# TensorE's 128-column work gathered into every second stage of a convolution-and-involution kernel

## The chip, the cores and the metric

The kernel runs on one core of one Trainium2 chip. The metric is device microseconds (us) of one execution, the median of several runs. Profiles are one execution each, by the hardware profiler. The engines are called PE (TensorE, the matrix engine; PEld is its weight load), DVE (VectorE), ACT (ScalarE), POOL (GpSimd) and SP (which here only issues DMAs).

## The reference

The input x is 32 images of 256 channels by 32x32 pixels, in float32. Two layers, each with a residual, where gn is a group norm with 32 groups of 8 channels:

```python
# layer 0: 3x3 convolution, 256 -> 256 channels, operands clipped to float16's range
x = x + conv3x3(quantize(gn(x)), quantize(weight)) + bias
# layer 1: involution; every pixel makes its own 7x7 kernel for each of 16 groups of 16 channels
z = gn(x)
y = relu(batchnorm(w1 @ z))               # 256 -> 64 channels, per pixel
w = w2 @ y + b2                           # 64 -> 16 groups * 49 taps, per pixel
x = x + sum over 49 taps of w[group, tap, pixel] * z[channel, pixel shifted by tap]
```

## The kernel before

The images go through a pipeline that is written out by hand: one Python loop (line 513) emits instructions for all engines, and each engine executes its own in the order in which they were emitted. The loop runs over **stages** n. An image has 16 of them: four blocks k of 8 image rows, times two sets v of columns of the 7x7 window (v=0: four columns, 128 partitions; v=1: three columns, 96 partitions), times two halves d of its rows (d=0: four, d=1: three). I number them 0 to 15 by n mod 16; k=0 is stages 0 to 3. In the iteration for stage n are emitted, in this order:

1. the *products* of stage n (`products`, L408): weights times shifted pixels, on DVE into tiles `pa` and `pb` and on POOL into `pg`. `pa` and `pb` have two buffers each, `pg` four;
2. the *sums* of stage n-1 (`sums`, L462): PE matmuls with a 32-column 0/1 matrix `shift`, four side by side in the array, that add the products up into `acc`. A stage with d=0 takes 32 of them in the trace, one with d=1 24, and the corner stages of k=0 fewer;
3. one step of `finish`, which closes a block of rows: ACT copies acc (`ob`, L473), PE transposes it with four 128-column matmuls (L479, in stages 1, 5, 9, 13), DVE adds it to x (L488, L491);
4. in even stages the *weights* for stages n+2 and n+3 (`weights`, L371): small 32-column matmuls into `pw` (64 in the trace for v=0, 48 for v=1), half of which ACT then copies to `ws` (L380) for POOL;
5. one step of every `front` that is running. A front is a generator, one for an image, started 38 stages before the image's stage 0; each `yield` ends a step, and each iteration runs one step of each live front, the oldest first.

A front's steps are these. The first group norm: sums (ACT, L195), means (PE `pg` matmul with `avg`, L203, and ACT, L210), squares (L195), variances (`pg` again, then `s` and `ve` on ACT, L220 and L222), scales (a reciprocal `r` on DVE, L226), and apply, a run of ten small and large ACT instructions (L231 to L243) that writes `xq`. Then the convolution in four units of 18 matmuls (L287, 128x128 weights, 512 columns moving, float16), each spread over four steps by `CONV = (0, 6, 4, 8)`; after a unit come the clip `q` on DVE (L301), `qb` on ACT (L303), the residual `x` on POOL (L305) and ACT's sums of it. Then the second group norm, whose apply writes `xn`; four steps with four transposes each (`pt`, L324), a copy by ACT (`xt4`, L328) and four DMAs (L330) that store the normalized image by pixels in DRAM; `load_pixels` (L359), which loads it to `xpix`; and `py` (L337, 64 columns) with ACT's relu into `y_pad` (L345). The tile `m` in PSUM, which pg, pt and py share, has one buffer.

In the steady state three fronts are live: that of image b+1 is in its second group norm and transposes while b+2 is convolved and b+3 begins. The second norm's variances are emitted in stage 4, its scales and apply in stage 5, the transposes in stages 6, 7, 8 and 9, load_pixels and py in stage 10. The first norm's apply is emitted in stage 0 and the convolution in stages 1 to 15.

Of the kernel before, what the change touches and what calls it, by code (L numbers as in the profile page):

```python
# [57 lines left out]
def tile_quant_conv_then_involution(  # L58
# [28 lines left out]
    def load_x(b):  # L87
        xt = xpool.tile([P, CH, N], F32, tag="x", name=f"x_{b}")
        for h in range(CH):
            nc.sync.dma_start(xt[:, h], x[b, h * P : (h + 1) * P])  # L90
        return xt
# [93 lines left out]
    class GroupNorm:  # L185
# [42 lines left out]
        def apply(self, dst, src):  # L228
# [10 lines left out]
            for h in range(CH):  # L239
# [8 lines left out]
                    scale=rstd[:, one],  # L248
                )


    CONV = (0, 6, 4, 8)

    def front(b):


        xt = x_tiles[b]
        gn = GroupNorm()
        gn.begin(1)
        for h in range(CH):  # L260
            gn.add_up(xt, 0, h, 0, N, AF.Identity)
        yield
        gn.means()
        gn.squares(xt)
        yield
        gn.variances()
        yield
        gn.scales()
        yield
        yield  # L270
        yield

        gn.apply(lambda h: xq[:, h, PAD0 : PAD0 + H, PAD0 : PAD0 + W], xt)
        yield
        gn = GroupNorm()
        gn.begin(N // NT)
        units = [(nt, mh) for nt in range(N // NT) for mh in range(CH)]
        for s in range(1, 4 * len(units) + 3):
            u, i = divmod(s, 4)
            if u < len(units):  # L280
                nt, mh = units[u]
                if i == 1:
                    pc = ps_c.tile([P, NT], F32, tag="pc", name="pc")
                for n in range(sum(CONV[:i]), sum(CONV[: i + 1])):
                    kh, k = divmod(n, K0 * K0)
                    i0, j0 = divmod(k, K0)
                    nc.tensor.matmul(  # L287
                        pc,
                        wq[:, kh, k, mh * P : (mh + 1) * P],
                        xq[:, kh, nt * RT + i0 : nt * RT + i0 + RT, j0 : j0 + W],  # L290
                        start=n == 0,
                        stop=n == CH * K0 * K0 - 1,
                    )

            u, i = divmod(s - 4, 4)
            if 0 <= u < len(units) and i < 3:
                nt, mh = units[u]
                cols = slice(nt * NT, (nt + 1) * NT)
                if i == 0:
                    q = work.tile([P, NT], F16, tag="q", name="q", bufs=1)  # L300
                    nc.vector.tensor_scalar(q, pc, F16_MAX, -F16_MAX, ALU.min, ALU.max)  # L301
                    qb = work.tile([P, NT], F32, tag="qb", name="qb", bufs=1)
                    nc.scalar.activation(qb, q, AF.Identity, bias=bias_sb[:, mh : mh + 1])  # L303
                elif i == 1:
                    nc.gpsimd.tensor_tensor(xt[:, mh, cols], qb, xt[:, mh, cols], ALU.add)  # L305
                else:
                    gn.add_up(xt, nt, mh, nt * NT, (nt + 1) * NT, AF.Identity)
            yield
        gn.means()
        gn.squares(xt)  # L310
        yield
        gn.variances()
        yield
        gn.scales()
        xn = work.tile([P, CH, N], F32, tag="xn", name=f"xn_{b}", bufs=1)
        gn.apply(lambda h: xn[:, h].rearrange("p (r c) -> p r c", c=W), xt)
        yield

        xd = pixels[b] = dram.tile([W, H, C], F32, tag="xd", name=f"xd_{b}")
        for r in range(0, H // 4, 2):  # L320
            pt = ps_m.tile([P, 2, C], F32, tag="m", name="pt")
            for s in range(2):
                for h in range(CH):
                    nc.tensor.transpose(  # L324
                        pt[:, s, h * P : (h + 1) * P], xn[:, h, (r + s) * P : (r + s + 1) * P], ident
                    )
            xt4 = work.tile([P, 2, C], F32, tag="xt4", name="xt4")
            nc.scalar.copy(xt4, pt)  # L328
            for i in range(4):
                nc.sync.dma_start(xd[:, 4 * r + i : 4 * r + i + 5 : 4, :], xt4[i * W : (i + 1) * W])  # L330
            yield
        load_pixels(b, 0)

        py = ps_m.tile([P, NT], F32, tag="m", name="py")
        for kh in range(CH):
            for nt in range(N // NT):
                nc.tensor.matmul(  # L337
                    py[nt * CR : (nt + 1) * CR],
                    w1_sb[:, kh, :],
                    xn[:, kh, nt * NT : (nt + 1) * NT],  # L340
                    start=kh == 0,
                    stop=kh == CH - 1,
                )
        for nt in range(N // NT):
            nc.scalar.activation(  # L345
                y_pad[b % 2][:CR, nt * RT : (nt + 1) * RT, PAD1 : PAD1 + W],
                py[nt * CR : (nt + 1) * CR].rearrange("p (r c) -> p r c", c=W),
                AF.Relu,
                bias=bn_shift,
                scale=bn_scale,  # L350
            )
        yield

    def load_pixels(b, i):

        for r0, r1 in (((0, 7), (15, 22), (7, 15)), ((0, 14), (14, 22)))[i]:
            src = HELD[i][r0]
            for q in range(Q):
                nc.sync.dma_start(  # L359
                    xpix[i][q * W : (q + 1) * W, r0:r1], pixels[b][:, src : src + r1 - r0, :]  # L360
                )
# [92 lines left out]
    def sums(acc, v, d, moves):  # L454
        p = W * len(COLS[v])
        most = max(len(m) for m in moves)
        for i in range(most):
            for t in range(T):
                if i < len(moves[t]):
                    moving, of = moves[t][i]  # L460
                    cols = slice(0, NT) if of == 2 else slice(of * C, (of + 1) * C)
                    nc.tensor.matmul(  # L462
                        acc[t * W : (t + 1) * W, cols],
                        shift[v][:p],
                        moving,
                        start=(v, d, i) == (0, 0, 0),
                        stop=(v, d, i) == (len(COLS) - 1, len(DI) - 1, len(moves[t]) - 1),
                    )
# [39 lines left out]
    with tc.manual_schedule():  # L508
        fronts, done = {}, {}
        ending = iter(())  # L510
        acc = last = None
        pws = {}
        for n in range(FRONT, len(stages) + 3):
            if 0 <= n < len(stages):
                b, k, v, d = stages[n]
                now = stages[n], products(b, k, v, d, *pws[n // 2])
            else:
                now = None
            if last is not None:
                (b, k, v, d), prods = last  # L520
                if (v, d) == (0, 0):
                    acc = ps_acc.tile([P, NT], F32, tag="acc", name="acc")
                sums(acc, v, d, prods)
            next(ending, None)
            if last is not None and (v, d) == (len(COLS) - 1, len(DI) - 1):
                ending = finish(b, k, acc)
                next(ending)
            last = now
            b, at = divmod(n, per)
            if at == 0 and 0 <= b < B:  # L530
                load_pixels(b, 1)
            if 0 <= n + 2 < len(stages) and n % 2 == 0:
                pws.pop(n // 2 - 1, None)
                pws[n // 2 + 1] = weights(*stages[n + 2][:3])
            b, at = divmod(n - LOAD, per)
            if at == 0 and 0 < b < B:
                x_tiles[b] = load_x(b)
            b, at = divmod(n - FRONT, per)
            if at == 0 and 0 <= b < B:
                fronts[b] = front(b)  # L540
                done[b] = 0
            for b in list(fronts):
                due = n - FRONT - b * per + 1
                if b == 1:

                    due = min(due, max(0, 2 * (due - HOLD)))
                while b in fronts and done[b] < due:
                    if next(fronts[b], fronts) is fronts:
                        fronts.pop(b)
                    done[b] += 1  # L550


# [34 lines left out]
```

## Time and profile before

| | us |
|---|---|
| median of 3 runs | 2783.15 (2783.02 to 2784.85) |
| the profiled execution | 2785.05 |
| its span, first to last instruction | 2783.3 |
| PE, POOL, DVE, ACT busy | 2721.5, 2576.7, 2478.3, 1048.0 |
| from one image's py to the next one's, image after image | 84.25 |

The granted PE clock is 0.991 over the span. "Busy" of PE is the union of its matmuls, whose ends are modelled and overlap, so starts are a better guide: the text that follows goes by the starts of matmuls in the timeline. A merged row of the timeline gives the start of the first instruction, the time from there to the end of the last one, the instruction and how many.

### The profile page before, as it was taken

To read this page: it belongs to the slowest core of one execution; us is meant where nothing else is said; L and a number is where in the kernel's file an instruction comes from. 1 tells how busy PE (TensorE), PEld (TensorE's weight loads), DVE (VectorE), ACT (ScalarE), POOL (GpSimd) and SP (SyncE) were. 2 spreads that over 40 slices of the span, in tenths; PEclk is the share of its full clock that TensorE was granted. 3 is DMA by queue.
4 is the path that set the end of the run, shared out by engine and by line. 5 is a ranking of instruction groups with operands and counts; after the bars stand their busy time and mean duration, and the time that the engine had idled before them with its cause. 6 is when DMAs were issued, how large, how long until landed. Compare 5 with 4: busy or idle time off the path is not lost.

```text
span 2783.3 us, 73320 instructions
## 1 busy us (share of the span) xinstructions
PE 2721.5 (98%) x32320; PEld 1222.7 (44%) x32320; DVE 2478.3 (89%) x1451; ACT 1048.0 (38%) x2179; POOL 2576.7 (93%) x857
## 2 busy tenths in 40 slices
PE   5999999999999999999999999999999999999998
PEld 2444444444444444444444444444444444444443
DVE  1799999999999999999999999999999999999898
ACT  5443344343343433343433343433433433434210
POOL 2799999999999999999999999999999999999997
PEclk8999999999999999999999999999999999999999
DMA  2555434355344454343454343454343453443440
GB/s 94 116 121 128 99 89 116 96 121 122 96 100 104 107 122 113 94 111 91 116 126 109 89 118 87 121 128 98 90 115 96 122 121 96 102 102 93 107 115 16
DMA packets 99853, 292.60 MB, mean 105 GB/s; under 512 B 21389, under 2 KB 62349, under 8 KB 86990
## 3 DMA queue, kind: packets, MB, share of 16 engines
q1 hardware_dynamic: 99534, 287.93, 42.5%
q8 instruction: 252, 4.13, 0.7%
q14 instruction: 67, 0.55, 0.1%
HBM read 220.73 MB, written 67.11 MB: 103 GB/s over the span
## 4 chain that ended last, share of the span: by engine, by line
PE 90%; ACT 4%; issue 2%; POOL 2%; DMA 1%; DVE 1%; POOLq 0%; SPq 0%; ACTq 0%; DVEq 0%
PE acc L462 50%; PE pc L287 18%; PE pw L371 13%; PE pt L324 2%; PE py L337 2%; PE acc L479 2%; POOL pg L408 2%; PE pg L203 1%; ACT xq L243 1%; ACT qb L303 1%; ACT w L234 1%; DMA xpix<-xd 0%; DVE pa L408 0%; ACT u L236 0%; ACT off L242 0%
## 5 line engine op out<-in xcount | busy, mean ns | idle before, releaser
L408 POOL TENSOR_TENSOR pg<-ws,xpix 96x2048 f32<-96x2048 f32 (+2 forms) x704 | 2407.0, 3451 | 23.5 <-PE acc L462 17.6
L408 DVE TENSOR_TENSOR pa<-pw,xpix 128x4096 f32<-128x4096 f32 (+7 forms) x832 | 2006.2, 2446 | 223.1 <-ACT junk L195 86.9
L462 PE MATMUL acc<-pa,shift 128*32 128x512 f32 (+3 forms) x7680 | 1566.2, 570 | 6.9 <-DVE pa L408 6.8
L462 PE MATMUL acc<-pg,shift 128*32 128x512 f32 (+1 forms) x5248 | 1481.5, 599 | 6.3 <-POOL pg L408 6.3
L462 PEld LDWEIGHTS acc<-pa,shift 128*32 128x32 f32 (+1 forms) x7680 | 379.2, 110 | 807.4 <-issue 764.6
L287 PE MATMUL pc<-xq,wq 128*128 128x512 f16 x2304 | 576.8, 387 | 18.7 <-ACT xq L243 15.5
L462 PE MATMUL acc<-pb,shift 128*32 128x512 f32 (+1 forms) x1152 | 531.1, 597 | 0.8 <-DVE pb L408 0.8
L371 PEld LDWEIGHTS pw<-w_sb,y 65*32 65x32 f32 x14336 | 415.0, 110 | 140.6 <-issue 134.4
L371 PE MATMUL pw<-w_sb,y 65*32 65x112 f32 x14336 | 442.7, 260 | 0.0
L380 ACT COPY ws<-pw 128x448 f32<-128x448 f32 (+1 forms) x256 | 135.9, 531 | 724.7 <-PE pw L371 715.3
L462 PEld LDWEIGHTS acc<-pg,shift 128*32 128x32 f32 (+1 forms) x5248 | 354.9, 110 | 65.2 <-issue 51.2
L287 PEld LDWEIGHTS <-wq 128*128 128x128 f16 x2304 | 213.5, 99 | 311.1 <-issue 119.9
L408 DVE TENSOR_TENSOR pb<-pw,xpix 128x1536 f32<-128x1536 f32 x192 | 335.0, 1745 | 0.0
L305 POOL TENSOR_TENSOR x<-qb,x 128x512 f32<-128x512 f32 x128 | 164.4, 1285 | 169.7 <-ACT qb L303 154.4
L473 ACT COPY ob<-acc 128x512 f32<-128x512 f32 x128 | 75.1, 587 | 515.9 <-PE acc L462 514.5
L328 ACT COPY xt<-pt 128x512 f32<-128x512 f32 x128 | 75.0, 586 | 227.0 <-PE pt L324 125.8
L195 ACT ACTIVATE junk<-x 128x512 f16<-128x512 f32 (+1 forms) x192 | 147.9, 770 | 10.7 <-POOL x L305 6.2
L195 ACT ACTIVATE junk<-x,mean 128x1024 f16<-128x1024 f32 x128 | 147.2, 1150 | 4.1
L462 PEld LDWEIGHTS acc<-pb,shift 128*32 128x32 f32 (+1 forms) x1152 | 111.2, 109 | 8.5 <-issue 4.3
L301 DVE TENSOR_SCALAR q<-pc 128x512 f16<-128x512 f32 x128 | 87.0, 680 | 31.3 <-PE pc L287 31.3
L479 PEld LDWEIGHTS acc<-ident,ob 128*128 128x128 f32 x512 | 53.6, 140 | 108.1 <-issue 82.2
L303 ACT ACTIVATE qb<-q,bias_sb 128x512 f32<-128x512 f16 x128 | 92.5, 722 | 11.8 <-DVE q L301 11.8
(51 smaller groups left out, 975.1 us busy)
## 6 DMA issues: line engine op xcount, KB each, us to landing
xpix<-xd SPq DMA_DIRECT2D x256, 256.0 KB, 10.0
xpix<-xd SPq DMA_DIRECT2D x256, 224.0 KB, 5.1
xpix<-xd SPq DMA_DIRECT2D x128, 448.0 KB, 6.6
x<-in_x SPq DMA_DIRECT2D x64, 512.0 KB, 3.6
xd<-xt SPq DMA_DIRECT2D x512, 64.0 KB, 1.7
out<-x SPq DMA_DIRECT2D x32, 640.0 KB, 3.1
out<-x SPq DMA_DIRECT2D x32, 384.0 KB, 2.5
wf<-in_w SPq DMA_DIRECT2D x2, 1152.0 KB, 8.7
```

The costliest lines, as they stand in the source:

```text
L195: nc.scalar.activation(junk[:, n0:n1], src[:, h, n0:n1], func, bias=bias, accum_out=self.sums[:, part, h : h + 1])
L287: nc.tensor.matmul(pc, wq[:, kh, k, mh * P : (mh + 1) * P], xq[:, kh, nt * RT + i0 : nt * RT + i0 + RT, j0 : j0 + W], start=n == 0, stop=n ...
L301: nc.vector.tensor_scalar(q, pc, F16_MAX, -F16_MAX, ALU.min, ALU.max)
L303: nc.scalar.activation(qb, q, AF.Identity, bias=bias_sb[:, mh : mh + 1])
L305: nc.gpsimd.tensor_tensor(xt[:, mh, cols], qb, xt[:, mh, cols], ALU.add)
L328: nc.scalar.copy(xt4, pt)
L371: nc.tensor.matmul(pw[q * W : (q + 1) * W, r // 4, o : o + K1 * G], y_pad[b % 2][:, ROWS[k][r], s : s + W], w2_sb[:, dj, :], start=True, s ...
L380: nc.scalar.copy(ws[:p], pw[:p, 1, : 4 * K1 * G].rearrange("p (r m) -> p r m", r=4))
L408: eng.tensor_tensor(o, win, xin, ALU.mult)
L462: nc.tensor.matmul(acc[t * W : (t + 1) * W, cols], shift[v][:p], moving, start=(v, d, i) == (0, 0, 0), stop=(v, d, i) == (len(COLS) - 1, l ...
L473: nc.scalar.copy(ob, acc.rearrange("p (r c) -> p r c", c=C))
L479: nc.tensor.transpose(po[:, h, :, r, :], ob[:, r, h * P : (h + 1) * P], ident)
```

## The change

`CONV` becomes (0, 9, 0, 9): a unit's 18 matmuls go 9 and 9 into two odd stages. Empty steps move the variances of both group norms one step later (into stages 13 and 5) and the scales behind them (for the first norm stage 14, for the second stage 6, with its apply). A step may now yield `MORE`, upon which the next live front has its turn and the first one then goes on within the same iteration; so two groups of transposes are emitted in stage 7 and two in stage 9, each pair with the other image's convolution in between. load_pixels stays in stage 10 and py goes to stage 11. Nothing is computed differently.

```diff
-    CONV = (0, 6, 4, 8)
+    MORE = 1
+
+    CONV = (0, 9, 0, 9)
...
         gn.means()
         gn.squares(xt)
         yield
+        yield
         gn.variances()
         yield
         gn.scales()
-        yield
         yield
         yield
...
         gn.means()
         gn.squares(xt)
         yield
+        yield
         gn.variances()
         yield
         gn.scales()
...
-            yield
+
+            if r % 4 == 0:
+                yield MORE
+            else:
+                yield
+                if r == 2:
+                    yield
         load_pixels(b, 0)
+        yield
...
-            for b in list(fronts):
+            for b in list(fronts) * 2:
...
-                    if next(fronts[b], fronts) is fronts:
+                    got = next(fronts[b], fronts)
+                    if got is fronts:
                         fronts.pop(b)
+                    elif got == MORE:
+                        break
                     done[b] += 1
```

So on PE, with the other engines' instructions left out, a period of 16 stages changes from the left column to the right one ("conv 6" is six convolution matmuls; acc-T, pt and py are four instructions each in the program):

| stage | before | after |
|---|---|---|
| 0 | sums, weights | sums, weights |
| 1 | sums, acc-T, conv 6 | sums, acc-T, conv 9 |
| 2 | sums, weights, conv 4 | sums, weights |
| 3 | sums, pg, conv 8 | sums, pg, conv 9 |
| 4 | sums, weights, pg | sums, weights |
| 5 | sums, acc-T, conv 6 | sums, acc-T, pg, conv 9 |
| 6 | sums, weights, pt, conv 4 | sums, weights |
| 7 | sums, pt, conv 8 | sums, pt, conv 9, pt |
| 8 | sums, weights, pt | sums, weights |
| 9 | sums, acc-T, pt, conv 6 | sums, acc-T, pt, conv 9, pt |
| 10 | sums, weights, py, conv 4 | sums, weights |
| 11 | sums, conv 8, pg | sums, py, conv 9, pg |
| 12 | sums, weights, pg | sums, weights |
| 13 | sums, acc-T, conv 6 | sums, acc-T, conv 9, pg |
| 14 | sums, weights, conv 4 | sums, weights |
| 15 | sums, conv 8 | sums, conv 9 |

## The prediction

> **What bounds the kernel now.** I read the page's busy line first, then the chain that ended last, then the busy time inside one period.
>
> ```profile
> PE 2721.5 (98%) x32320; PEld 1222.7 (44%) x32320; DVE 2478.3 (89%) x1451; ACT 1048.0 (38%) x2179; POOL 2576.7 (93%) x857
> PE 90%; ACT 4%; issue 2%; POOL 2%; DMA 1%; DVE 1%; POOLq 0%; SPq 0%; ACTq 0%; DVEq 0%
> ```
>
> ```profile
> core 0: us, PE busy (x) PEld busy (x) DVE busy (x) ACT busy (x) POOL busy (x), PEclk, DMA share, GB/s
> 1407.39:1491.64 84.25, 84.09 (x1014) 37.90 (x1010) 77.30 (x46) 32.62 (x68) 80.17 (x27) 1.00 0.44 108
> ```
>
> The second fence is one image, from py to py. PE is busy 84.09 of 84.25 us and the chain is 90% PE, so in the steady state PE's instruction stream sets the pace; POOL follows with 4.1 us to spare per image, DVE with 6.9. ACT has much idle time, but it works in order, and its place in the order will matter. The period repeats to 0.001 us, so what one period gains or loses counts some 30 times.
>
> **What a switch costs.** The timeline of PE, stages 6 and 7:
>
> ```profile
> 1467.61 1.72 PE L371 MATMUL pw<-w_sb,y 65*32 65x112 f32 x64
> 1469.26 0.66 PE L324 MATMUL pt<-ident,xn 128*128 128x128 f32 x4
> 1469.75 1.04 PE L287 MATMUL pc<-xq,wq 128*128 128x512 f16 x4
> 1470.72 0.62 PE L462 MATMUL acc<-pa,shift 96*32 96x512 f32 x2
> ...
> 1473.76 0.60 PE L462 MATMUL acc<-pg,shift 96*32 96x512 f32 x2
> 1474.29 0.66 PE L324 MATMUL pt<-ident,xn 128*128 128x128 f32 x4
> 1474.79 1.93 PE L287 MATMUL pc<-xq,wq 128*128 128x512 f16 x8
> 1476.65 0.62 PE L462 MATMUL acc<-pa,shift 96*32 96x512 f32 x2
> ```
>
> The reader is to see the starts where the array changes from 32 columns to 128 and back. Four sums side by side recur every 0.43 us, and weights after sums start 0.41 after the last sum; a 128-column matmul starts 0.52 after it (1473.77 to 1474.29): 0.11 more. A convolution matmul takes 0.2215 (1.55 for seven steps); sums after it start 0.31 later (0.09 more). Around weights the clearest price is a whole block. The 4 convolution matmuls of stage 14 stand between the last weight matmul (row 1428.43, 1.72, less 0.26 for one: 1429.89) and the first sum at 1431.07: 1.17 us. Where nothing stands between (stage 0: last weights 1440.56, last sums 1443.67, which with a switch come 3.05 after the first), the gap is worth 0.06. So the block costs 1.11, of which the matmuls are 0.89: 0.22 to 0.24 for entering and leaving. The diff takes 7 of 15 such blocks out of a period: 7 x 0.24 = 1.7 us.
>
> **The sum of PE's work, stage by stage.** Taken out of even stages, each the gap after the weights less 0.06: stage 2 (conv 4) 1.12; 4 (pg) 0.45; 6 (pt, conv 4) 1.60; 8 (pt) 0.72; 10 (py, conv 4) 2.98; 12 (pg) 0.45; 14 1.12. Together 8.44. Put into odd stages, beside matmuls of 128 columns: 16 convolution matmuls x 0.2215 = 3.54; pt behind the convolution in 7 and 9, twice 0.50 (0.22 + 0.38 + 0.20 to the sums, less the 0.31 that stands there now); pg in 5 some 0.24 and in 13 0.12; py in 11 1.87 (1.35 and 0.52 to the convolution). Together 6.77. Net -1.7 us a period, 82.6 in place of 84.25, the same as by counting blocks.
>
> The Trainium skill, "TensorEngine Tiling (Array Packing)", Key Properties, says that changing the tiling mode drains the engine; the rows show such a cost. "TensorE: Matmul & The Clock Gate", Single matmul latency, puts the constant part of an isolated matmul at about 166 ns with a warm clock; as an estimate, two such drains a block would be 0.33 and seven blocks 2.3 us, with which the whole sum below would end 19 us lower, at about 2778, on the edge of no change. The rows have the same thing at 0.24, and I go by them.
>
> **What goes wrong: the second norm's apply.** The rows of ACT in the same stages (5 and 6):
>
> ```profile
> 1462.92 0.20 ACT L231 ACTIVATE t<-r 128x2 f32<-128x2 f32 x1 [2.07 <-DVE r L226]
> ...
> 1466.44 1.25 ACT L243 ACTIVATE xn<-x,off,rstd 128x1024 f32<-128x1024 f32 x1
> 1469.45 0.53 ACT L380 COPY ws<-pw 128x448 f32<-128x448 f32 x1 [1.76 <-PE pw L371]
> 1469.95 0.59 ACT L328 COPY xt<-pt 128x512 f32<-128x512 f32 x1
> ```
>
> Now apply is emitted in stage 5, runs 1462.92 to 1467.69 (4.77 us) while PE does sums and weights, and the first transposes, at 1469.26, find xn finished 1.6 us before. In the changed program the scales and apply belong to stage 6. There the weights come before the fronts, so on ACT the copy ws stands ahead of t, and ws waits for PE's weights of that stage. Counted from the start of the last weight matmul of stage 6 (now 1469.07): ws starts at +0.38; what stands behind a ws that waits for nothing begins at +0.81 (stage 14: 1430.70 against 1429.89); xn's second half ends at +0.81 + 4.77 = +5.58; the second transpose, which reads it, starts some 0.15 later (weight load and matmul), +5.73. On PE only 32 sums now lie between: 0.06 + 3.05 + 0.52 + 0.13 = +3.76. So PE stands about **1.97 us** in every period. Behind the waiting transposes are 9 convolution matmuls, the second pt and the sums of the next stage: all of PE. No cover is left; ACT's idle time does not help, since t may not pass ws. The cost is bounded below by 1.5 (if the copy's end and the loading overlap better) and above by 2.3.
>
> Net per period: -1.7 + 1.97 = +0.28, 84.5 us. Image 1's to image 30's periods have both parts (30 times): **+8.5 us**.
>
> **The rest of what moves.** First-norm scales move to stage 14 and apply stays in stage 0, behind the same ws and qb: the existing 0.33 stall of the convolution on xq (1445.01) stays. Variances leave stages 4 and 12, so s and ve no longer stand between ws and qb there: qb 0.3 earlier, no loss. r moves behind DVE's products of stage 6; by the sums above it is ready 1.7 us before t can run. py and relu come a stage later, first read by the weights of stage 14: 3 stages of cover. SP issues the same DMAs; the last four xd stores come behind the convolution of stage 9, some 2.5 us later, and the loads follow them; DVE's stage 0 is over 20 us behind (1434.80 against 1411), covered. PSUM's `m`: the second pt of a pair waits for ACT's copy of the first (0.7 us), under 2.0 us of convolution.
>
> POOL: the residual add, at 1.6 after the last weights of stages 0, 4, 8 and 12, leads 8.58 us later to the second pg of the next d=0 stage (1421.45 to 1430.03). PE will reach stage 15 at 10.4 after the weights of stage 12, POOL at 10.2: it holds by 0.2. At stage 7 it is a tie (stages 1 to 4 take PE 18.2, POOL 18.65), but a stall of 0.1 there is absorbed by the wait for xn.
>
> **Before the first products** (two views, ACT then SP):
>
> ```profile
> 57.35 0.20 ACT L231 ACTIVATE t<-r 128x2 f32<-128x2 f32 x1
> ...
> 62.01 0.71 ACT L303 ACTIVATE qb<-q,bias_sb 128x512 f32<-128x512 f16 x1
> 62.85 0.59 ACT L328 COPY xt<-pt 128x512 f32<-128x512 f32 x1
> ```
>
> ```profile
> 63.46 7.51 SPq L330 DMA_DIRECT2D xd<-xt  x16
> 71.01 15.63 SPq L359 DMA_DIRECT2D xpix<-xd  x20
> ```
>
> Here the chain is serial: image 0's xn, transposes, 16 stores, loads, first product at 85.96. Changed, the variances' pg stands behind 18 convolution matmuls of image 1 instead of 6 (end about 59.4, now 56.4), and qb ahead of t: t at 61.2 instead of 57.35, +3.8. The last pt waits for one more 9-matmul block, +0.7. I take **+4.5 us** (bounds 2 and 7). After the last convolution the end of the run is limited by POOL and DVE (PE waits 2.9 at 2632.0), where PE's wait for xn mostly disappears: +0.5 (0 to 2).
>
> **Sum:** 8.5 + 4.5 + 0.5 = +13.5. The profiled execution took 2785.05 (2783.3 and 1.75 around it), 1.9 above the median; added to the median 2783.15 it is **2796.7 us**, 0.5% slower.
>
> **Rivals.**
>
> 1. *The wait for xn does not come* (faster). For it: now xn is 1.6 us early, and ACT is idle 62%. It decides if t starts before +0.81 - 1.97, that is over a microsecond before ws can. Against: ACT's order. Then 30 x -1.7 + 5 = -46: 2737. 10%.
> 2. *Nearly balanced*: the wait is at its lower bound, or a switch is worth 0.30 instead of 0.24. Net between -0.15 and +0.05 a period: 2783 to 2789. 15%.
> 3. *POOL takes over*: it is busy 80.2 of 84.5; if its adds come 0.6 late, the margin of 0.2 at stage 15 becomes a stall of 0.4 or more per period: 2809 and up, to 2820. 8%.
> 4. *It does not do what it says*: the switches cost the same wherever the work stands, and only the wait is new: 30 x 1.97 + 5 = +64: 2847. The rows around stage 0 speak against it. 2%.
>
> **Numbers.** My forecast, 2789 to 2808, has 65%. The range 2780 to 2812 takes in the second case and the near part of the third; about 15% lies outside. A difference under 0.2% (5.6 us) cannot be told from none. Faster by more: rival 1 and a little of 2, 12%. Within: the rest of 2, some of the low end of mine, 16%. Slower: 72%.
>
> **What would show it.** Right: the first transposes' idle time ends with ACT's xn, about 2 us, some 31 times; a period of 84.5 with PE busy 82.5; after weights a sum follows at once in every even stage; first product near 90.4. Wrong: a period near 82.6 (no wait), or PE waiting for pg in stages 7 or 15, or DVE's r later than ws.

## The result, and the profile after

The changed kernel takes 2789.58 us (median of 6 runs, 2781.03 to 2789.92), the kernel before 2783.84 beside it (6 runs, 2782.77 to 2785.2): ratio 1.0016, 95% interval 1.0003 to 1.0028. It is slower by 5.7 us, about at the bound of what can be told from no change; the forecast was 13.5 us. The profiled execution took 2789.92, with a span of 2788.2 (before: 2783.3).

The page's busy line and the chain that ended last:

```profile
PE 2685.1 (96%) x32320; PEld 1323.7 (47%) x32320; DVE 2484.6 (89%) x1451; ACT 1052.4 (38%) x2179; POOL 2575.8 (92%) x857
PE 85%; ACT 10%; issue 2%; POOL 1%; DMA 1%; DVE 1%; POOLq 0%; SPq 0%; ACTq 0%; DVEq 0%
```

PE is busy 36 us less, and the chain's share of PE falls from 90% to 85%, while ACT's rises from 4% to 10%. Something on ACT now decides where PE used to. One period, from py to py, in the busy time of each engine:

```profile
core 0: us, PE busy (x) PEld busy (x) DVE busy (x) ACT busy (x) POOL busy (x), PEclk, DMA share, GB/s
1417.13:1501.34 84.21, 82.77 (x1014) 41.21 (x1010) 77.50 (x46) 32.78 (x69) 80.14 (x27) 1.00 0.45 108
```

The period is 84.213 us (84.253 before): PE is busy 1.3 us less in it and stands 1.44 us, before 0.16. Where it stands is seen in PE's timeline of stages 6 and 7:

```profile
1388.35 1.72 PE L380 MATMUL pw<-w_sb,y 65*32 65x112 f32 x64
1389.88 0.60 PE L471 MATMUL acc<-pa,shift 96*32 96x512 f32 x2
...
1393.73 0.33 PE L326 MATMUL pt<-ident,xn 128*128 128x128 f32 x1
1395.44 0.55 PE L326 MATMUL pt<-ident,xn 128*128 128x128 f32 x3 [1.38 <-ACT xn L243]
1395.82 2.15 PE L288 MATMUL pc<-xq,wq 128*128 128x512 f16 x9
1397.80 0.60 PE L326 MATMUL pt<-ident,xn 128*128 128x128 f32 x4
1398.33 0.62 PE L471 MATMUL acc<-pa,shift 96*32 96x512 f32 x2
```

The sums now follow the weights at once. The first transpose runs, the second waits for `xn`: it starts 1.71 us after the first instead of 0.11. ACT in the same stretch:

```profile
1390.18 0.53 ACT L389 COPY ws<-pw 128x448 f32<-128x448 f32 x1 [5.92 <-POOL pg L417]
1390.61 0.21 ACT L231 ACTIVATE t<-r 128x2 f32<-128x2 f32 x1
...
1394.14 1.24 ACT L243 ACTIVATE xn<-x,off,rstd 128x1024 f32<-128x1024 f32 x1
```

ACT stands idle 5.92 us ahead of `ws`, then `t` follows 0.43 later and the second half of `xn` ends at 1395.38, 5.58 after the last weight matmul (1389.80), as the prediction had it. (The idle time of `ws` is put down to POOL's pg, which ended at about the same time; the copy reads `pw`, and starts 0.38 after the last weight matmul, as it did before.)

The way to the first products, ACT and then SP:

```profile
62.35 0.19 ACT L231 ACTIVATE t<-r 128x2 f32<-128x2 f32 x1
...
68.09 0.58 ACT L330 COPY xt<-pt 128x512 f32<-128x512 f32 x1 [0.38 <-PE pt L326]
```

```profile
68.70 10.27 SPq L332 DMA_DIRECT2D xd<-xt  x16
79.01 16.89 SPq L368 DMA_DIRECT2D xpix<-xd  x20
```

`t` comes 5.0 us later than before and the stores 5.2; POOL's first product starts at 90.12 (before: 86.01), and the sums of stage 1 at 104.50 (98.37).

The span's 4.9 us can be followed by PE's transposes of acc in stage 1. In image 1 they come 5.5 us later than before (180.39 and 185.92), in image 29 4.4 later (2539.48 and 2543.88), and the span ends 4.9 later: +5.5 from the start, 28 x -0.04 = -1.1 in the periods, +0.5 at the end.

### The profile page after: what moved, and what is told of

It reads as the page before. It is cut to its first block, busy times and chain, and to the rows that moved or that the text cites. A ratio compares the mean times of both kernels' runs of the same rounds, so it can differ in the third digit from the quotient of the medians.

```text
span 2788.2 us, 73320 instructions
## 1 busy us (share of the span) xinstructions
PE 2685.1 (96%) x32320; PEld 1323.7 (47%) x32320; DVE 2484.6 (89%) x1451; ACT 1052.4 (38%) x2179; POOL 2575.8 (92%) x857
## 4 chain that ended last, share of the span: by engine, by line
PE 85%; ACT 10%; issue 2%; POOL 1%; DMA 1%; DVE 1%; POOLq 0%; SPq 0%; ACTq 0%; DVEq 0%
PE acc L471 46%; PE pc L288 18%; PE pw L380 13%; ACT xn L243 3%; PE pt L326 2%; PE py L346 2%; PE acc L488 2%; ACT xq L243 1%; POOL pg L417 1%; ACT w L234 1%; PE pg L203 1%; ACT off L242 1%; ACT rstd L241 1%; ACT qb L304 1%; ACT u L236 1%
## 5 line engine op out<-in xcount | busy, mean ns | idle before, releaser
L471 PE MATMUL acc<-pg,shift 128*32 128x512 f32 (+1 forms) x5248 | 1503.2, 599 | 5.5 <-POOL pg L417 5.5
L471 PEld LDWEIGHTS acc<-pa,shift 128*32 128x32 f32 (+1 forms) x7680 | 394.9, 110 | 558.8 <-issue 497.8
L288 PE MATMUL pc<-xq,wq 128*128 128x512 f16 x2304 | 556.3, 387 | 15.6 <-ACT xq L243 10.7
L471 PEld LDWEIGHTS acc<-pg,shift 128*32 128x32 f32 (+1 forms) x5248 | 457.1, 111 | 162.0 <-issue 141.5
L288 PEld LDWEIGHTS <-wq 128*128 128x128 f16 x2304 | 221.2, 100 | 300.8 <-issue 81.5
L326 PE MATMUL pt<-ident,xn 128*128 128x128 f32 x512 | 86.8, 283 | 47.4 <-ACT xn L243 45.3
L220 ACT ACTIVATE s<-pg,eps 128x2 f32<-128x2 f32 x64 | 16.8, 262 | 238.5 <-PE pg L203 238.5
```

Of the source, the lines that this page charges most:

```text
L288: nc.tensor.matmul(pc, wq[:, kh, k, mh * P : (mh + 1) * P], xq[:, kh, nt * RT + i0 : nt * RT + i0 + RT, j0 : j0 + W], start=n == 0, stop=n ...
L326: nc.tensor.transpose(pt[:, s, h * P : (h + 1) * P], xn[:, h, (r + s) * P : (r + s + 1) * P], ident)
L471: nc.tensor.matmul(acc[t * W : (t + 1) * W, cols], shift[v][:p], moving, start=(v, d, i) == (0, 0, 0), stop=(v, d, i) == (len(COLS) - 1, l ...
```

## The experiments

All ratios are to the kernel before, run on the same chip at the same time (its medians there: 2784.8 to 2785.1). "Period" is the mean from py to py over the middle images of the run's trace, and lengths are from the starts of matmuls. Where two experiments are set against each other, the kernels before that ran beside them differ by at most 0.4 us; beside the changed kernel it took 2783.84, up to 1.3 less.

**The theory:** PE's own work falls by about 1.9 us a period because 128-column blocks are joined, and PE's wait for `xn`, which comes from the place of the second norm's apply behind `ws` in ACT's order, gives it back. **Rivals:** the switches cost nothing and the times come from elsewhere; the wait comes from the variances' being a stage later, or from POOL.

**1. Apply back in stage 5, everything else as changed.**

```diff
         gn.variances()
-        yield
         gn.scales()
         xn = work.tile([P, CH, N], F32, tag="xn", name=f"xn_{b}", bufs=1)
         gn.apply(lambda h: xn[:, h].rearrange("p (r c) -> p r c", c=W), xt)
         yield
+        yield
```

> The changed kernel, with the second norm's scales and apply emitted in stage 5 again, right behind the variances, so that ACT does them ahead of the copy ws of stage 6; transposes stay in stages 7 and 9. Theory (the gain of the gathered blocks is eaten by the wait for xn behind ws): the wait of 1.6 us at the first transposes goes, the wait for POOL's pg of 0.3 in stage 7 stays; period 84.21 - 1.6 = 82.6 us, total 2789.6 - 48 = 2741 us. Rival (POOL takes over as soon as PE is faster): period 83.3 or more, total 2762 or more, with PE waiting for pg. Rival (gathering is worth nothing): period 84.2, total 2789.

Measured: 2738.41 us, ratio 0.9831 (0.9817 to 0.9844); period 82.625.

```profile
1222.36:1304.98 82.62, 82.55 (x1014) 41.06 (x1010) 77.51 (x46) 32.89 (x69) 80.14 (x27) 1.00 0.45 110
```

PE is busy for all but 0.07 us of this kernel's period. Its timeline in stages 6 and 7:

```profile
1277.79 1.72 PE L380 MATMUL pw<-w_sb,y 65*32 65x112 f32 x64
1279.32 0.60 PE L471 MATMUL acc<-pa,shift 96*32 96x512 f32 x2
1279.34 0.91 PE L471 MATMUL acc<-pg,shift 96*32 96x512 f32 x2
...
1282.34 0.90 PE L471 MATMUL acc<-pg,shift 96*32 96x512 f32 x2
1283.18 0.65 PE L326 MATMUL pt<-ident,xn 128*128 128x128 f32 x4
1283.67 2.15 PE L288 MATMUL pc<-xq,wq 128*128 128x512 f16 x9
```

The four transposes run together, with no wait. The variances were still a stage later than before the change, so that is not the cause. One wait stays: the 32 sums of stage 7 take 3.33 us from first to last start, in both kernels. Without a wait it is 3.05 where a 128-column block stands between the weights and the sums (every such stage of the kernel before), and 3.03 where the sums follow the weights at once, as here (stages 11 and 15). So they stand 0.30 for POOL's second `pg`: the rows of two `pg` matmuls are 0.9 long for 0.6, as the second starts 0.30 behind the first. Without this wait the period would be 82.32, that is 1.93 below 84.253: this is the change in PE's work alone. (The sums of stage 1 also wait for POOL, 0.10, and the wait for `xq` behind them, 0.33 before, is as much shorter, 0.23.)

**2. The convolution alone as 9 and 9, in the kernel before.**

```diff
-    CONV = (0, 6, 4, 8)
+    CONV = (0, 9, 0, 9)
```

> The kernel before with CONV = (0, 9, 0, 9) alone: the convolution leaves stages 2, 6, 10 and 14, but 6 and 10 keep pt and py, so two 128-column blocks a period go, in stages 2 and 14. Theory (a block's entry and exit cost 0.24 us): period 84.25 - 0.47 = 83.8 us, total 2784 - 14 = 2770 us. Rival (switches cost the same wherever the work stands): 84.25, 2784 us.

Measured: 2771.12 us, ratio 0.9952 (0.9939 to 0.9964); period 83.672, 0.58 below before. Stage 14 in this kernel:

```profile
1256.56 1.72 PE L371 MATMUL pw<-w_sb,y 65*32 65x112 f32 x64
1258.09 0.60 PE L462 MATMUL acc<-pa,shift 96*32 96x512 f32 x2
```

Two blocks (stages 2 and 14) disappear wholly, at 0.24 each: the stretch from the last weight matmul to the first sum of stage 14 shrinks by 1.095 and the sums behind it by 0.02 (3.03 for 3.05), while the 4 matmuls that go to stages 13 and 15 add 0.662 and 0.215. Stage 10, where `py` stays, gives another 0.11, since the convolution behind `py` had an entrance of its own: 0.24 + 0.24 + 0.11 = 0.59, measured 0.58. So this half of the change gains without any wait.

**3. The second norm's scales and apply a stage later, in the kernel before.**

```diff
         gn.variances()
+        yield
         gn.scales()
```

> The kernel before with one empty step between the second norm's variances and scales: scales and apply move to stage 6, behind ws, transposes to 7, 8, 9 and 10, py to 11; as many blocks of 128 columns as before. Theory (apply behind ws is late): xn's second half is ready 5.6 us after the last weight matmul of stage 6, the second transpose would start 4.9 after it (4 convolution matmuls lie between): a wait of 0.75 to 0.85 us a period, total 2784 + 24 = 2808 us. Rival (ACT's order does not matter, the loss lies elsewhere): 2784 to 2786 us.

Measured: 2813.4 us, ratio 1.0102 (1.0088 to 1.0116); period 85.142, +0.89. This kernel's PE timeline at the first transposes:

```profile
1320.02 0.33 PE L325 MATMUL pt<-ident,xn 128*128 128x128 f32 x1
1320.92 0.55 PE L325 MATMUL pt<-ident,xn 128*128 128x128 f32 x3 [0.57 <-ACT xn L243]
```

The second transpose is 0.79 late (0.90 behind the first instead of 0.11), within the expected 0.75 to 0.85. The wait is shorter than in the changed kernel by the four convolution matmuls that still stand between here; the yield also puts the transposes and py a stage later, which is worth the other 0.1. The apply's move by itself costs time.

**4. The old start, everything else as changed.** The fronts of images 0 and 1 keep the old steps, all later ones the new.

```diff
+        old = b < 2
+        conv = (0, 6, 4, 8) if old else CONV
...
-        yield
+        if not old:
+            yield
         gn.variances()
```

> The changed kernel, with the fronts of images 0 and 1 as in the kernel before. Theory (the start costs 5 to 6 us because image 0's second norm and stores stand behind more of image 1's convolution): the first product comes as early as before, total 2789.6 - 5.5 = 2784 us, period unchanged at 84.21. Rival (the later start is chance, from the clock granted in the first 100 us): 2789 us.

Measured: 2780.35 us (11 runs, 2775.02 to 2786.55), ratio 0.9984 (0.9974 to 0.9994), so 9 us under the changed kernel, where 5 to 6 were expected. The runs of this one program differ by more than those of any other, and go with the mean granted clock: 2785.9 to 2786.6 at 0.990 (three runs), 2780.4 to 2781.5 at 0.991 (three), 2775.0 to 2777.3 at 0.992 to 0.994 (five). The changed kernel had 0.990 in five of its six runs and 0.994 in the sixth, 2781.03. At equal mean clock the two kernels are 3.4 us (0.990) and some 4 us (0.994) apart, and by this measure that is what the changed start costs. That the rest is clock is argued, not shown: an equal mean does not say that the half-clock stretches fall at the same places.

**5. One convolution matmul per unit back in the even stage, in the kernel of experiment 1.**

```diff
-    CONV = (0, 9, 0, 9)
+    CONV = (0, 8, 1, 9)
```

> The kernel of e1_apply5 (2738.4, period 82.63) with one thing undone: of each unit's 18 convolution matmuls one goes back to the even stage before (8, 1, 9 in place of 9, 9), so that 4 blocks of 128-column work of a single matmul stand again behind the weights of stages 2, 6, 10 and 14. The amount of work is the same. If entering and leaving the 128-column mode costs 0.22 to 0.25 us per block, the period grows by 4 x 0.235 = 0.94, to 83.56, and the time to 2738 + 28 = 2766 (2763 to 2769). If a switch costs nothing and e1_apply5 gains by something else: 2738.

Measured: 2756.49 us, ratio 0.9897 (0.9884 to 0.9911); period 83.280, +0.655 and not +0.94. A block of one matmul in this kernel's PE timeline:

```profile
1248.18 1.72 PE L380 MATMUL pw<-w_sb,y 65*32 65x112 f32 x64
1249.83 0.39 PE L288 MATMUL pc<-xq,wq 128*128 128x512 f16 x1
1250.15 0.62 PE L471 MATMUL acc<-pa,shift 96*32 96x512 f32 x2
```

From the last weight matmul (1249.64) to the first sum it takes 0.51; without the block 0.08. (1249.64 is the row's start and length less 0.26 for one matmul.) That is 0.434 more, and the sums behind the block take 0.024 longer (3.05 for 3.03); of this the matmul itself is 0.217 (saved in the odd stage): 0.24 for the two switches, as expected. Four of them are 0.96. But the sums of stage 7 now take 3.05, their length behind a block: the wait of 0.30 for POOL has gone, as PE comes later. 0.96 - 0.30 = 0.66. (In stage 1 the wait for `xq` grows by 0.10 and that for POOL's products goes, 0.10.) So switches do cost, and part of what a faster PE gains here is lost to POOL.

**6. Experiment 1 with the old start of experiment 4.**

> The kernel of e1_apply5 with the steps of the fronts of images 0 and 1 as they were before the change (only the way to the first products is undone). If the way to the first products costs what e4_oldstart gained on the changed kernel (9 us): about 2729; by the later start in the changed kernel's trace (5.5 to 6.1 us): 2732 to 2733. If the start is hidden behind something that comes after it: 2738. The period should stay at 82.63.

Measured: 2734.51 us, ratio 0.9821 (0.9807 to 0.9834); period 82.625, 3.9 us under experiment 1 (3.8 between their runs of clock 0.992). Both profiled executions have nearly the same time at half clock before POOL's first product (table below), which starts at 81.30 here and at 85.66 there, 4.4 apart. PE's transposes of acc are then 5.3 to 5.4 apart in every image up to the last; over its last transposes experiment 6 has 3.4 us more at half clock (from 2712.7), and only 3.9 remain. So the changed start costs 4 to 5 us.

**7. The fronts' step ahead of the weights, in every stage of the changed kernel.** PE's own order is not altered, but ACT's apply stands ahead of `ws`.

```diff
-            if 0 <= n + 2 < len(stages) and n % 2 == 0:
-                pws.pop(n // 2 - 1, None)
-                pws[n // 2 + 1] = weights(*stages[n + 2][:3])
...
                     done[b] += 1
+            if 0 <= n + 2 < len(stages) and n % 2 == 0:
+                pws.pop(n // 2 - 1, None)
+                pws[n // 2 + 1] = weights(*stages[n + 2][:3])
```

> The changed kernel with the fronts' step emitted ahead of the weights in every stage; the order of PE's own instructions stays that of the changed kernel, but ACT's apply no longer stands behind the copy ws. If the wait of PE in stage 7 comes from that place in ACT's order, as the theory has it, it goes for the most part (1.6 to 1.9 us a period, and the 0.33 us before the convolution of stage 1 as well): 2735 to 2750, if the later ws costs POOL nothing. If POOL, which gets its ws of stage 6 up to 3 us later, then sets the pace: 2750 to 2800. If PE's wait has another cause (the variances a stage later, DVE's r), nothing changes: 2789.

Measured: 2817.23 us, ratio 1.0116 (1.0102 to 1.013); period 85.28. This is above all three cases. Both waits for ACT are gone (the four transposes run in 0.38, the convolution of stage 1 starts 0.11 after the transposes of acc ahead of it), but POOL's waits in one period read:

```profile
POOL pg L417 <- ACT ws L389: 3.8, 1, 3.8
```

Once a period POOL stands 3.8 us for the `ws` of stage 0, which now comes behind the first norm's apply. By the profile DVE stands for the same copy, and PE then for DVE (two views, DVE and PE):

```profile
1290.61 3.68 DVE L417 TENSOR_TENSOR pa<-pw,xpix 96x768 f32<-96x768 f32 x6 [2.50 <-ACT ws L389]
```

```profile
1299.27 0.62 PE L471 MATMUL acc<-pa,shift 96*32 96x512 f32 x2 [0.73 <-DVE pa L417]
```

PE waits 0.8 for DVE's `pa` ahead of the sums of stage 4, and in the sums of stages 5, 7, 9 and 11 1.1, 0.9, 0.3 and 0.2 by the lengths of their runs, while POOL, late by its 3.8, works with one pause of 0.9.

**8. Experiment 6 with the fronts first as well.**

> e6_apply5_oldstart with the fronts' step ahead of the weights as well, as in e7_fronts_first. What it can still gain over e6_apply5_oldstart is the 0.33 us a period that the convolution of stage 1 waits for the first norm's apply behind ws: 10 us, so about 2720 to 2723. If POOL's later ws costs as much: no gain or a loss, 2730 to 2760.

Measured: 2802.34 us, ratio 1.0063 (1.005 to 1.0075); period 84.80. A miss as in 7, for the same reason: POOL stands 3.8 us for the same `ws`, and PE waits 0.8 us ahead of the sums of stage 4 and 1.1 and 0.9 in those of stages 5 and 7.

**9. The fronts' step ahead of the weights in stage 6 alone.** The edit of 7, with `n % per == 6` in its condition, and the weights of other stages where they were.

> The changed kernel with one edit: in stage 6 alone the fronts' step is emitted ahead of the weights, so that the second norm's apply stands ahead of that stage's ws on ACT; stage 0 and all others stay as in the changed kernel (in e7_fronts_first, where all stages were turned round, POOL stood 3.8 us a period for the ws of stage 0). If the place of apply behind ws is the whole cause of PE's wait at the first transposes, that wait (1.60 us a period) goes, and if POOL has room for a ws of stage 6 that comes 3.6 us later, the period is that of e1_apply5, 82.63, and the time 2789.6 - 30 x 1.59 = 2742. If POOL has no such room (pace set by POOL): part of it comes back, 2745 to 2790. If the cause lies elsewhere (variances a stage later): 2789.

Measured: 2782.06 us, ratio 0.9991 (0.9982 to 1.0); period 84.05. PE's timeline of stages 7 and 9 in this kernel, and then ACT's of stages 6 and 7:

```profile
1301.19 0.66 PE L326 MATMUL pt<-ident,xn 128*128 128x128 f32 x4
...
1309.57 0.62 PE L471 MATMUL acc<-pg,shift 128*32 128x512 f32 x1 [0.21 <-POOL pg L417]
```

```profile
1299.77 1.24 ACT L243 ACTIVATE xn<-x,off,rstd 128x1024 f32<-128x1024 f32 x1
...
1301.54 0.51 ACT L389 COPY ws<-pw 128x448 f32<-128x448 f32 x1
```

`xn` is ready 0.2 us before the transposes, and their wait of 1.60 is gone. `t` ran as soon as DVE's `r` was there, 1.0 us ahead of the last weight matmul, where in the changed kernel it ran 0.81 behind it. That shows the cause: the same instructions on PE, and only the place in ACT's order altered. But `ws` starts 4.28 after the last weight matmul (1297.26) instead of 0.38; POOL, which reads it, stands 1.8 us, and the sums of stage 9 take 4.24 to 4.27 instead of 3.02. With 0.18 in stage 11 and less in others, 1.4 of the 1.6 comes back. ACT cannot serve both in time: the room has to be found a stage earlier, as in experiment 1.

**10. Experiment 6 with the first norm's apply in stage 15 instead of 0.**

```diff
         gn.scales()
         yield
-        yield
         gn.apply(lambda h: xq[:, h, PAD0 : PAD0 + H, PAD0 : PAD0 + W], xt)
         yield
+        yield
```

(for the images from the third on)

> e6_apply5_oldstart (2734.5) with the first norm's apply moved from stage 0 to stage 15, where no weights stand ahead of it. The convolution of stage 1 then no longer waits for xq: 0.23 us a period less, 30 x 0.23 = 7, about 2727.5. Against it: apply must wait for the convolution of stage 15 that still reads xq, and the ws of stage 0 then stands behind apply; in e7_fronts_first a late ws of stage 0 cost 3.2 us a period through POOL. If POOL becomes late by this: 2740 to 2800.

Measured: 2725.67 us, ratio 0.9792 (0.9778 to 0.9805), the fastest of all; period 82.49.

```profile
1214.95:1297.43 82.48, 82.48 (x1014) 40.66 (x1011) 77.43 (x46) 32.89 (x69) 80.11 (x27) 1.00 0.45 110
```

The wait in stage 1, 0.21 in experiment 6, is gone; 0.07 of it comes back in the sums of stage 7, whose wait for POOL grows from 0.30 to 0.37.

| | period | from before | us |
|---|---|---|---|
| before | 84.253 | | 2783.84 |
| changed | 84.213 | -0.04 | 2789.58 |
| 1: apply in stage 5 | 82.625 | -1.63 | 2738.41 |
| 2: convolution 9 and 9 alone | 83.672 | -0.58 | 2771.12 |
| 3: apply later alone | 85.142 | +0.89 | 2813.4 |
| 4: old start | 84.218 | -0.04 | 2780.35 |
| 5: as 1, convolution 8, 1, 9 | 83.280 | -0.97 | 2756.49 |
| 6: as 1, old start | 82.625 | -1.63 | 2734.51 |
| 7: fronts first | 85.28 | +1.03 | 2817.23 |
| 8: as 6, fronts first | 84.80 | +0.55 | 2802.34 |
| 9: fronts first in stage 6 | 84.05 | -0.20 | 2782.06 |
| 10: as 6, apply in stage 15 | 82.49 | -1.76 | 2725.67 |

## Why the prediction was wrong in its size

The direction, the wait and its place were right. The step that failed is this one: "Net per period: -1.7 + 1.97 = +0.28, 84.5 us". Measured, it is -1.94 + 1.90 = -0.04. In the period no mechanism was missing: two terms of nearly equal size were off in the same direction, PE's work by 0.24 and the wait by 0.07, and 30 periods made 9.6 us of it. This is more than the 7.8 us that the forecast was off; the rest of the sum came out 1.8 dearer. That the slower start, and not the period, makes the result slower was not forecast: +8.5 of the +13.5 were to come from the periods, which give -1.3.

- **PE's work, -1.7 by stages, measured -1.94.** What was taken out of even stages is right: 8.44 in all, as forecast. The odd stages, forecast at 6.77, take 6.51. (8.44 less 6.77 is 1.67; with it the prediction's own sum would have been +0.30 and not +0.28.) They were priced too high where an instruction joins a block that is there already: pg in stage 5 costs 0.14, not 0.24; pt behind the convolution in 7 and 9 costs 0.44, not 0.50, each; the convolution's 16 matmuls 3.51, not 3.54. Experiment 1 gives the same 1.93 with the wait taken away. The counting by blocks (7 x 0.24) agreed with the sum by stages, and that looked like a confirmation. Experiments 2 and 5 do put a block at 0.24; what it leaves out is that joining within the odd stages saves more.
- **The wait, 1.97, measured 1.90.** `xn` ended at +5.58 as forecast, and the first sums and transpose were priced to 0.02; the second transpose started at +5.64, not +5.73, so the 0.15 from `xn` to it was 0.06. Of the 1.90, 0.30 are the sums of stage 7, which wait for POOL: the tie that the prediction saw there. It is absorbed by the wait for `xn`, as was said; but it stays when that wait goes (experiment 1), so that moving apply back gives 1.60 and not 1.90.
- **The cause of the wait** is ACT's order: shown by experiments 1, 3 and 9. The Trainium skill, "TensorE: Matmul & The Clock Gate", Architectural detail, calls ACT's queue strictly first in, first out; the rows agree: experiment 9 shows that `t` could have run 1.8 us earlier, and in the changed kernel ACT stood idle there with `ws` at the head.
- **The start, +4.5.** Profile against profile the sums of stage 1 come 6.1 later and the transposes of acc in stage 1 of the next image 5.5; experiments 4 and 6 put the changed start at 3.4 to 5.4 us. So the size was about right, but the path was misread, and luck is in it. The prediction let image 0's loads release the first product at 85.96. In the trace before, the eighth load lands at 81.53, and DVE's first product starts 0.03 after the copy `ws`, which waits for PE's weights, and these run at half clock (the window is from 78.49 to 88.73). Weights and copy before, and the weights in experiment 4, at full clock:

```profile
82.12 3.22 PE L371 MATMUL pw<-w_sb,y 65*32 65x112 f32 x64
85.40 0.53 ACT L380 COPY ws<-pw 128x448 f32<-128x448 f32 x1 [5.34 <-PE pw L371]
```

```profile
78.63 1.74 PE L389 MATMUL pw<-w_sb,y 65*32 65x112 f32 x64
```

In the changed kernel DVE's first product again follows `ws` and starts at 87.56, where the prediction looked for 90.4; POOL's, at 90.12, follows the eighth load, which lands at 89.96, 8.4 later than before and not 4.5. `t` came 5.0 later, for the forecast 3.8. At equal half-clock time the load is indeed 4.4 to 4.5 later (81.0 and 81.1 in experiments 4 and 6, 85.4 and 85.5 in 9 and 1).
- **The end, +0.5:** measured 0.5, by the transposes of acc above. The profile after also has 3.5 us more at half clock there (27.5 for 24.0), so what part is the end's own stays open.
- **The rivals.** The second, nearly balanced, is what happened (net between -0.15 and +0.05), though for neither of its two reasons: the wait was not at its lower bound, nor a switch dearer. The measured time is also at the lowest edge of the main forecast, 2789 to 2808. The first gave 2737 if no wait came; experiment 1, which takes the wait away, has 2738.4. The third did not come in stage 15; POOL's limit shows in stage 7 with 0.30 and in stage 1 with 0.10, and decides in experiments 7 to 9. The fourth falls with experiments 2 and 5.
- **The rule on drains.** The prediction set an estimate of 0.33 per block from the Trainium skill beside 0.24 from the rows; experiments 2 and 5 measure 0.24, and the rows decide.

What stays open is 1 to 3 us of the 5.7: start, periods and end together explain some 3 to 5, and the rest is put down to the half-clock stretches of the first 100 and the last 160 us, of which no run had control.

## What to carry to other kernels

When a forecast is the small difference of two large terms that repeat in every period, give each term its own error and let the range, not the middle, speak: 0.1 us in a term of 1.9 was 3 us here, and the sign of the whole hung on it. Before instructions are moved to another step, read what stands ahead of them in the order of every engine that they use: the gain on PE was real (46 us in experiment 1), and one copy that waits ahead of an apply took all of it. And when the first bound is relieved, look at the next engine's place in the same stretch: POOL, 4 us of slack in the period, was late in single stages as soon as its `ws` moved.

## What the runs showed of the hardware

In the first 100 us the granted clock falls to half in several windows, and where these fall differs between kernels with the same start; between runs of one program the mean clock differs. Up to POOL's first product the profiles have these times at half clock (worked out from the granted clock in steps of 2 us from 38 us on):

| kernel | us at half clock before it | POOL's first product at |
|---|---|---|
| before | 24.6 | 86.01 |
| 4 (old start) | 17.6 | 81.15 |
| 6 (old start) | 17.3 | 81.30 |
| changed | 23.9 | 90.12 |
| 9 (new start) | 17.1 | 85.52 |
| 1 (new start) | 17.1 | 85.66 |

Some seven us more at half clock go with a first product that is 4.5 to 4.9 later, for either start; at some 17 us of it, the new start is 4.2 to 4.5 later than the old one. The last 160 us have such windows too: 24.0 us in all before, 27.5 in the changed kernel, 15.3 in experiment 1. One of 3.4 us stands in the middle of experiment 4's profile, from 1637.1: PE's transposes of acc are 11.1 us earlier than the changed kernel's up to there and 9.45 behind it, so that 3.4 us at half clock cost 1.65 where PE sets the pace.

Two stretches of the changed kernel and then of experiment 1, busy times and, third from the end, the granted clock:

```profile
60.00:66.00 6.00, 3.55 (x17) 1.53 (x15) 0.76 (x2) 4.46 (x13) 1.27 (x1) 1.00 0.00 0
66.00:72.00 6.00, 4.85 (x14) 2.37 (x15) 0.00 (x0) 2.29 (x4) 0.00 (x0) 0.51 0.18 44
```

```profile
60.00:66.00 6.00, 4.28 (x20) 1.90 (x20) 0.00 (x0) 4.48 (x9) 1.24 (x1) 1.00 0.00 0
66.00:72.00 6.00, 4.48 (x24) 2.20 (x22) 0.69 (x1) 2.99 (x6) 1.29 (x2) 1.00 0.35 89
```

The half-clock window follows a stretch in which PE was busy 3.55 of 6 us, and does not come after 4.28 of 6. That it is the gap which brings the window is only argued from such pairs; no run varied it alone, and the busy share alone does not order them: in experiment 2 a stretch of 3.41 us (89.02 to 92.43) with PE busy 2.04 is followed by half clock, in experiment 1 one (86.93 to 90.34) with 1.99 is not. The Trainium skill, "TensorE: Matmul & The Clock Gate", What's actually happening, describes a gate that opens and closes by a window of some 3.4 us that runs free of the kernel, and says that its effect varies by run. The runs agree: the half-clock windows in the traces last 3.4, 6.8, 10.2 and 17.1 us, and experiment 4's program took 2775.0 to 2786.6 us with mean clocks of 0.994 to 0.990. For a change of 0.2% this is the larger part of the scatter, and kernels are best compared at equal mean clock, which still leaves open where the clock was lost.
